# Two layers of graph attention in one launch: who copies the encoder's denominators, where the last attention's small tiles live, and in which order layer 1's squares and relus run

## The chip, the core and the metric

The kernel runs on one NeuronCore of a Trainium2 chip. A core has five engines that run side by side, each with its own queue of instructions in a fixed order: TensorE (PE in the profile, PEld its weight loads), VectorE (DVE), ScalarE (ACT), GpSimd (POOL) and SyncE (SP), the last two of which here mostly issue DMA transfers. Engines wait for each other through semaphores. The metric is the device time of one launch in microseconds; the median of three runs of the kernel before is 3309.0 us (3308.68 to 3311.59).

## What is computed

The graph has 4096 nodes with 512 features and an adjacency matrix of zeros and ones. Layer 0 is an encoder and a decoder with the same attention weights, each followed by a multilayer block with batch norm; layer 1 is a graph attention of four heads. Cut to what matters:

```python
# layer 0: h = relu(layernorm(x)), four heads of 128 features
Xw  = einsum('hnd,hde->hne', Xh, W)
sig = sigmoid(f1[:, :, None] + f2[:, None, :])       # f1, f2: Xw against two vectors per head
att = masked_softmax(adj * sig, adj != 0)            # rows sum to 1
Xc  = concat(att @ Xw)                               # encoder's attention
emb = mlp_block(batchnorm(Xc))
out = mlp_block(elu((att @ emb) @ W.T))              # decoder: the same att again
x   = x + out
# layer 1: h = relu(layernorm(x)), four heads
feats  = einsum('nf,hfo->hno', h, W1)
logits = leaky_relu(e_s[:, :, None] + e_n[:, None, :], 0.2)
x = x + relu(softmax(logits where adj else -1e10) @ feats + b)
```

## The kernel before

**Attention.** The function `attention` (line 210) is called three times: "enc", "dec" and "gat". It runs over 8 blocks, one for each head h and each half tb of the target nodes (2048 columns). A block has NJ = 32 steps, one for each 128 source nodes. In a step, ScalarE makes the unnormalised weights e of 128 sources by 2048 targets (lines 419 and 420 for enc and dec, line 798 for gat), VectorE multiplies them by the mask a (line 421 or 799), and TensorE adds four products of 512 columns to the output (line 351; line 348 for the first two steps of the fourth output bank). An f32 matmul stands as two records in the trace. The tiles e rotate through a fixed set of buffers: eight in the encoder, so that step j + 8 writes the buffer that step j used.

**Denominators.** The encoder and gat also need the sum of e over all sources. It is formed in three ways, by the tables at lines 62 to 64: some steps go to TensorE as products with ones (line 303), eleven of 32 are added up in memory by accumulating transfers that GpSimd issues (line 363, `acc<-e` in the encoder), the others are added by VectorE (lines 369 and 371). At the end of a block TensorE adds the three parts into one PSUM bank, `den`. Each accumulating transfer is issued after the one before it has landed. The buffer of e is free only once its transfer has landed.

**The end of a block, spread over the next.** At step 2 of the next block the output banks are copied out (line 520, VectorE). At step 4, `denominators` (line 244) copies `den` to SBUF, sends it to memory and back through GpSimd's queue (lines 248 and 250), and at step 10 it is inverted (line 254). The inverse comes back spread over partitions (line 261) and scales the outputs. In the encoder, every fifth e is stored for the decoder, which reads it back.

**Order.** A framework turns the Python order into one fixed order of instructions for each engine and lets a pool's tile wait for what used its memory before. `tc.issue_after(x)` and `pinned(list)` hold instructions behind others on this order.

**Layer 1's projection.** Line 705, `centred(ib)`, works on 512 nodes: it subtracts the mean over features (line 714), takes the relu into hT for TensorE (line 717), the square (line 719), and sums the squares over features (line 720). TensorE then forms the mean square (line 726), from which `deviation` makes the scale of the evictions (line 748). TensorE's projection is line 743. Small tiles are in the pools `l_small` and `l_work`, closed before the pool "gat" is opened on the same memory.

**Entry of the last attention.** Lines 762 to 789 find the largest score, broadcast it (mbc), exponentiate columns (jcol), sum the features (line 776), and store the target rows g (line 789) for later blocks. Row 0 is made ready inside the first step (lines 796 and 797), in four parts.

Of the kernel before, what the change touches and what calls it, by code (L numbers as in the profile page):

```python
# [80 lines left out]
def kernel(ctx, tc, x, xT, adjT, w0, w0T, v0, wencT, wdecT, vecs, w1, w1T, a1, outT):  # L81
# [21 lines left out]
    def bank1():  # L103
        return psum1.tile([P, IB], FP, name="den")
# [70 lines left out]

        return pv[:, 0:2 * DX].rearrange("p (h x) -> p h x", x=DX)

    def store_rows(dst, src):

        n = src.shape[-1]  # L180
        pr = bank1()
        nc.tensor.transpose(pr[0:n, 0:P], src, ident)
        fr = consts.tile([P, P], FP, name="fr")
        nc.vector.tensor_copy(fr[0:n, :], pr[0:n, 0:P])
        nc.scalar.dma_start(dst.rearrange("h (q p) -> (h q) p", p=P), fr[0:n, :])

    def targets(tb):
        return score[:, 0, tb].rearrange("p h q -> p (h q)")
# [21 lines left out]
    def attention(what, keep, pools, weights, values, row_of, out, finish, ebufs, modes=None, invert=None,  # L210
# [33 lines left out]
        def denominators(h, tb, den):  # L244

            dsb = spool.tile([P, IB], FP, name="dsb")
            nc.scalar.copy(dsb, den)
            nc.gpsimd.dma_start(dens[h][tb], dsb[0:P:32, :])
            dcol = spool.tile([P, TB // P], FP, name="dcol", bufs=2)
            nc.gpsimd.dma_start(dcol, dens[h][tb].rearrange("s (q k) -> (s q) k", k=TB // P))  # L250
            return dcol
# [41 lines left out]
        for n, (h, tb) in enumerate(blocks):  # L293
# [15 lines left out]
            for j in range(NJ):  # L309

                with pinned(products_of):
                    for f in later.pop(j, []):
                        f()
                with tc.issue_after(a_load.ins) if j else nullcontext():
                    if (n, j) in extras:
                        extras[n, j](a_load)
                    if not last and j == NJ - 10:
                        next_row = next_row_of(*blocks[n + 1])
                if n == 0 and moved and j == NJ - 2:
                    back = weight_tile()  # L320
                    nc.gpsimd.dma_start(back, dacc)
                e = weight_tile()
                store = j % KEEP == KEEP - 1 and kept is not None
                if store and kept == "read":
                    a_load = nc.sync.dma_start(e, ekeep[h][tb][j // KEEP])
                else:
                    if masks0:
                        a, a_load = masks0.pop(0)
                    else:
                        a = mask_tile(keep)  # L330
                        a_load = load_mask(a, tb, j)
                    products_of = weights(e, rowb, a, j, h, SB if n + j == 0 else 1)
                    if store:
                        stores.append((j // KEEP, e))

                    if j % KEEP == KEEP - 3 and stores:
                        k, t = stores.pop()
                        nc.scalar.dma_start(ekeep[h][tb][k], t)

                def products():  # L340
                    nonlocal last_main, last_ones

                    with tc.issue_after(last_ones.ins) if last_ones is not None else nullcontext():

                        if j == EVICT:
                            po.append(bank())
                            for k, t in ahead:
                                nc.tensor.matmul(po[-1], block(values[h], k), t[:, (SB - 1) * IB:SB * IB],  # L348
                                                 start=(k == 0), stop=False)
                        for s, b in enumerate(po):  # L350
                            last_main = nc.tensor.matmul(b, block(values[h], j), e[:, s * IB:(s + 1) * IB],  # L351
                                                         start=(j == 0), stop=(j == NJ - 1))
                    last_ones = None


                early = last and j == NJ - 1 and invert is not None
                if not early:
                    products()
                if j < EVICT:
                    ahead.append((j, e))  # L360
                if invert is not None:
                    if j in moved:
                        nc.gpsimd.dma_start(sums2 if n else dacc, e, **({"accum_op": ALU.add} if j > moved[0] else {}))  # L363
                    elif j in by_ones:
                        held.append(e)
                    else:
                        adds.append(e)
                        if len(adds) == 2:
                            nc.vector.tensor_add(acc, *adds)
                        elif len(adds) > 2:  # L370
                            nc.vector.tensor_add(acc, acc, e)  # L371

                    if held and j + 1 not in by_ones:
                        with tc.issue_after(last_main.ins):
                            for t in held:
                                add_to_den(t)
                        held = []
                    if j == NJ - 1:
                        with tc.issue_after(last_ones.ins) if last_ones is not None else nullcontext():
                            if moved:  # L380
                                add_to_den(sums2 if n else back)
                            add_to_den(acc, True)
                if early:
                    products()
# [260 lines left out]


    v1 = xd
    with tc.tile_pool(name="l_small", bufs=1) as small, tc.tile_pool(name="l_work", bufs=2) as work:
        x1 = [R[2]] + [small.tile([P, N], FP, name=f"x1_{o}") for o in range(1, C)]

# [49 lines left out]
            nc.vector.tensor_copy(w1x[:, :, :, D:DX], pw[:, 0:2 * C * H].rearrange("p (c h s) -> p c h s", h=H, s=2))  # L700
        mean_of = small.tile([P, P], FP, name="mean_of")
        nc.gpsimd.memset(mean_of, 1.0 / F)
        vacc = small.tile([P, H, D], FP, name="vacc")

        def centred(ib):

            if ib >= NIB // 2:
                residual(C - 2, ib)
            residual(C - 1, ib)
            pm = bank()  # L710
            nc.tensor.matmul(pm, mean_of, S[ib], start=True, stop=True)
            sq = work.tile([P, C, IB], FP, name="sq", bufs=1)
            for fb in range(C):
                nc.vector.tensor_sub(sq[:, fb, :], nodes(x1[fb], ib), pm)
            hT = work.tile([P, C, IB], FP, name="hT")
            for fb in range(C):
                nc.scalar.activation(hT[:, fb, :], sq[:, fb, :], AF.Relu)  # L717
            for fb in range(C):
                nc.scalar.activation(sq[:, fb, :], sq[:, fb, :], AF.Square)
            nc.vector.tensor_reduce(S[ib], sq.rearrange("p c n -> p n c"), AX.X, ALU.add)  # L720
            return hT

# [36 lines left out]
                row0 = w.rearrange("p c f -> p (c f)")  # L759
                load_row(row0, rows1[0], 0)  # L760

        mloc = small.tile([P, H], FP, name="mloc")
        nc.vector.tensor_reduce(mloc, score[:, 1].rearrange("p t h q -> p h t q"), AX.XY, ALU.max)
        pt = bank1()
        nc.tensor.transpose(pt[0:H, 0:P], mloc, ident)
        mrow = small.tile([H, 1], FP, name="mrow")
        nc.vector.tensor_reduce(mrow, pt[0:H, 0:P], AX.X, ALU.max)
        mdiag = small.tile([H, H], FP, name="mdiag")
        nc.vector.tensor_scalar_mul(mdiag, ident[0:H, 0:H], mrow)
        pm = bank1()  # L770
        nc.tensor.matmul(pm[:, 0:H], ones[0:H, :], mdiag, start=True, stop=True)
        nc.vector.tensor_copy(mbc, pm[:, 0:H])

        pss = bank1()
        for h in range(H):
            last_sum = nc.tensor.matmul(pss[:, h:h + 1], vacc[:, h, :], ones[:, 0:1], start=True, stop=True)
        nc.vector.tensor_scalar_mul(ssum, pss[:, 0:H], TINY)
        mb = mbc.unsqueeze(1).unsqueeze(3).to_broadcast([P, NTB, H, NJ // NTB])
        nc.vector.tensor_sub(jcol, score[:, 1], mb)
        nc.scalar.activation(jcol2, jcol, AF.Exp, scale=0.2)  # L780
        nc.scalar.activation(jcol, jcol, AF.Exp)
        nc.vector.tensor_scalar_mul(nq, jcol2, -1.0)

        g = small.tile([P, NTB, H, NJ // NTB], FP, name="g")
        nc.vector.tensor_add(g, score[:, 0], mb)
        nc.vector.tensor_scalar_min(g, g, G_MAX)
        nc.scalar.activation(g, g, AF.Exp, scale=0.8)
        with tc.issue_after(last_sum.ins):
            store_rows(rowsg, g.rearrange("p t h q -> p (t h q)"))


    def gat_weights(e, rowb, a, j, h, parts):
        for e, rowb, a in in_parts(parts, e, rowb, a):

            if parts > 1:
                nc.vector.tensor_scalar(rowb, rowb, mbc[:, h:h + 1], G_MAX, ALU.add, ALU.min)
                nc.scalar.activation(rowb, rowb, AF.Exp, scale=0.8)
            last_act = nc.scalar.activation(e, rowb, AF.Relu, bias=column(nq, j, h), scale=column(jcol, j, h))  # L798
            last_dve = nc.vector.scalar_tensor_tensor(e, e, column(jcol2, j, h), a, ALU.add, ALU.mult)  # L799
        return last_act, last_dve  # L800
# [18 lines left out]
    with tc.tile_pool(name="gat", bufs=1) as spool:  # L819
        x1_last = []  # L820

        def load_last(load):
# [3 lines left out]
        attention("gat", spool, spool, gat_weights, v1, lambda h, tb: (rowsg, tb * H + h), out_gat,  # L826
                  (scaled_gat, add_to_output), 7, lambda n: GAT, (N * TINY, ALU.add), sums=R[2][:, 0:TB],
                  sums2=row0, row0=row0,
                  extras={(H * NTB - 1, NJ - 10): load_last})


def _inputs(x, adj, w):
# [39 lines left out]
```

## Time and profile before

The profiled run took 3310.35 us, with a span of 3308.6 us and a mean granted TensorE clock of 0.989. Busy times of stretches of the profile, in us:

| stretch (us from the start) | what | PE | DVE | ACT | DMA share |
|---|---|---|---|---|---|
| 452 to 574 (122) | one encoder block | 118.30 | 115.51 | 120.38 | 0.87 |
| 1500 to 2200 (700) | decoder's attention and the next block | 700.00 | 431.24 | 608.90 | 0.39 |
| 2200 to 2300 (100) | entry and first part of layer 1's projection | 93.79 | 70.64 | 62.14 | 0.23 |
| 2500 to 3000 (500) | last attention | 496.57 | 488.23 | 302.24 | 0.82 |

A stretch's busy time near its length marks an engine without slack there; three engines stand near it in the encoder. Matmuls are pipelined and their ends are modelled, so PE's figure overstates its load a little. Over the whole span PE is busy 98%, DVE 81%, ACT 79%.

### The profile page before, as it was taken

The numbers are of one execution on the slowest core, as the hardware profiler recorded it, in microseconds if no ns is written. First come the engines' busy times: TensorE is split into PE (matmuls) and PEld (weight loads), VectorE is DVE, ScalarE is ACT, GpSimd is POOL, SyncE is SP. The second block draws the span as 40 slices with busy tenths as digits, with TensorE's granted clock in tenths as the row PEclk, the third lists the DMA queues.
The fourth block names the chain that finished last, engine by engine and source line by source line (L and its number), as shares of the span: only waits on it lengthen the run. The fifth ranks groups of instructions, "written<-read, shape, count | busy, mean of one in ns | idle before, by whom it ended". The sixth has DMA issues, their size and how long they took to land.

```text
span 3308.6 us, 25868 instructions
## 1 busy us (share of the span) xinstructions
PE 3226.6 (98%) x8847; PEld 1492.2 (45%) x8847; DVE 2677.1 (81%) x1912; ACT 2602.9 (79%) x1908; POOL 329.1 (10%) x478
## 2 busy tenths in 40 slices
PE   7989999999999999999999999999999999999999
PEld 6434434434443464444444444448644444444443
DVE  6989899999998675555655666586599989999997
ACT  7999999999997448999999999565656566566563
POOL 2000110110110000000000000024201111111111
PEclk9999999999999999999999999999999999999999
DMA  9994888988986013333443443232389779778876
GB/s 207 196 187 147 249 225 231 248 224 227 248 238 186 4 45 137 135 129 137 152 140 124 137 153 133 66 134 75 82 199 223 174 194 221 192 193 208 216 190 147
DMA packets 180164, 558.54 MB, mean 169 GB/s; under 512 B 20356, under 2 KB 23684, under 8 KB 144192
## 3 DMA queue, kind: packets, MB, share of 16 engines
q0 software_dynamic: 43088, 210.09, 32.9%
q1 hardware_dynamic: 126288, 293.66, 26.2%
q10 hardware_dynamic: 10656, 53.15, 4.0%
q8 instruction: 69, 1.13, 0.1%
q14 instruction: 63, 0.52, 0.0%
HBM read 378.15 MB, written 95.82 MB: 143 GB/s over the span
## 4 chain that ended last, share of the span: by engine, by line
PE 67%; DVE 16%; issue 9%; ACT 5%; DMA 3%; DVEq 0%; ACTq 0%; POOL 0%; POOLq 0%
PE ps L351 52%; PE ps L566 7%; DVE e L421 4%; DVE e L799 4%; DVE R L371 4%; PE ps L743 3%; ACT e L419 2%; PE den L303 2%; DVE acc L371 2%; ACT e L420 2%; DMA a<-mask 2%; PE ps L622 1%; PE ps L348 1%; PE ps L500 1%; DMA rb<-rinvs 1%
## 5 line engine op out<-in xcount | busy, mean ns | idle before, releaser
L351 PE MATMUL ps<-e,R 128*128 128x512 f32 x6048 | 2640.7, 597 | 51.8 <-DVE e L421 39.9
L351 PEld LDWEIGHTS ps<-e,R 128*128 128x128 f32 x6048 | 1147.4, 191 | 1536.4 <-issue 1417.3
L421 DVE TENSOR_TENSOR e<-e,a 128x2048 f32<-128x2048 f32 (+1 forms) x470 | 1052.3, 2260 | 403.6 <-ACT e L420 381.6
L419 ACT ACTIVATE e<-rowb,score 128x2048 f32<-128x2048 f32 (+1 forms) x470 | 912.6, 1968 | 91.3 <-PE ps L351 58.0
L420 ACT ACTIVATE e<-e 128x2048 f32<-128x2048 f32 (+1 forms) x470 | 871.0, 1880 | 17.5 <-DVE e L421 11.1
L798 ACT ACTIVATE e<-rowb,nq,jcol 128x2048 f32<-128x2048 f32 x224 | 457.9, 2086 | 225.2 <-DMA w<-e 130.1
L799 DVE SCALAR_TENSOR_TENSOR e<-e,jcol,a 128x2048 f32<-128x2048 f32 (+1 forms) x259 | 591.5, 2319 | 4.5 <-DMA a<-mask 2.7
L371 DVE TENSOR_TENSOR R<-R,e 128x2048 f32<-128x2048 f32 x128 | 292.5, 2285 | 0.0
L371 DVE TENSOR_TENSOR acc<-acc,e 128x2048 f32<-128x2048 f32 x126 | 287.9, 2285 | 1.8
L566 PE MATMUL ps<-R,w 128*128 128x512 f32 x512 | 220.3, 592 | 0.6 <-DVE w L534 0.6
L261 POOL DMA_DIRECT2D rb<-rinvs x88 | 58.7, 683 | 1095.6 <-DVE R L524 904.8
L566 PEld LDWEIGHTS ps<-R,w 128*128 128x128 f32 x512 | 97.2, 190 | 122.7 <-issue 118.2
L363 POOL DMA_DIRECT2D w<-e x77 | 64.6, 839 | 643.6 <-DMA w<-e 267.5
L743 PE MATMUL ps<-w1x,hT 128*128 128x260 f32 x512 | 119.6, 393 | 1.8 <-ACT hT L717 1.8
L586 ACT ACTIVATE ex<-ps,bias 128x512 f32<-128x512 f32 x64 | 44.0, 688 | 95.5 <-PE ps L566 78.4
L363 POOL DMA_DIRECT2D acc<-e x66 | 55.6, 842 | 607.7 <-DMA acc<-e 225.7
L743 PEld LDWEIGHTS ps<-w1x,hT 128*128 128x128 f32 x512 | 99.2, 195 | 22.0 <-ACT hT L717 3.4
L798 ACT ACTIVATE e<-w,nq,jcol 128x2048 f32<-128x2048 f32 (+1 forms) x35 | 65.6, 1938 | 30.1 <-DMA dacc<-e 28.6
L811 ACT ACTIVATE R<-R,vec 128x512 f32<-128x512 f32 x32 | 23.0, 719 | 72.4 <-DVE R L808 72.3
L588 DVE SCALAR_TENSOR_TENSOR ex<-ex,re 128x512 f32<-128x512 f32 x64 | 45.0, 703 | 35.7 <-ACT re L587 35.5
L748 ACT ACTIVATE R<-ps,rstd 128x128 f32<-128x128 f32 x128 | 38.0, 367 | 42.4 <-PE ps L743 42.4
L303 PE MATMUL den<-e,ones 128*32 128x512 f32 x584 | 70.9, 599 | 0.0
(158 smaller groups left out, 1265.1 us busy)
## 6 DMA issues: line engine op xcount, KB each, us to landing
a<-mask SPq DMA_DIRECT2D x720, 256.0 KB, 3.5
w<-e POOLq DMA_DIRECT2D x77, 1024.0 KB, 8.2
acc<-e POOLq DMA_DIRECT2D x66, 1024.0 KB, 8.6
ekeep<-e ACTq DMA_DIRECT2D x48, 1024.0 KB, 5.5
e<-ekeep SPq DMA_DIRECT2D x48, 1024.0 KB, 4.9
rb<-rinvs POOLq DMA_DIRECT2D x88, 256.0 KB, 5.7
mask<-in_adjT POOLq DMA_DIRECT2D x8, 2048.0 KB, 103.3
rowb<-rows SPq DMA_DIRECT2D x16, 1024.0 KB, 4.9
```

What stands on the lines that cost most here:

```text
L261: nc.gpsimd.dma_start(rb, everywhere(rinvs[h][tb], 0, s * IB, IB))
L303: last_ones = nc.tensor.matmul(den[s * 32:(s + 1) * 32, :], ones[:, 0:32], t[:, s * IB:(s + 1) * IB], start=not begun, stop=stop)
L351: last_main = nc.tensor.matmul(b, block(values[h], j), e[:, s * IB:(s + 1) * IB], start=(j == 0), stop=(j == NJ - 1))
L363: nc.gpsimd.dma_start(sums2 if n else dacc, e, **({"accum_op": ALU.add} if j > moved[0] else {}))
L371: nc.vector.tensor_add(acc, acc, e)
L419: nc.scalar.activation(e, rowb, AF.Tanh, bias=column(score[:, 1], j, h), scale=0.5)
L420: last_act = nc.scalar.activation(e, e, AF.Exp, scale=0.5)
L421: last_dve = nc.vector.tensor_mul(e, e, a)
L566: nc.tensor.matmul(z, w[:, fb, o * P:(o + 1) * P], nodes(src[fb], ib), start=(fb == 0), stop=(fb == C - 1))
L743: nc.tensor.matmul(b[:, 0:2 * DX], hT[:, fb, c * P:(c + 1) * P], w1x[:, fb, 2 * k:2 * k + 2, :].rearrange("p h x -> p (h x)"), start=(fb = ...
L798: last_act = nc.scalar.activation(e, rowb, AF.Relu, bias=column(nq, j, h), scale=column(jcol, j, h))
L799: last_dve = nc.vector.scalar_tensor_tensor(e, e, column(jcol2, j, h), a, ALU.add, ALU.mult)
```

## The change

It has four parts. (1) In the encoder, the copy of `den` goes to VectorE instead of ScalarE; gat keeps ScalarE. (2) Small tiles that are used around the entry of the last attention (vacc, mloc, mrow, mdiag, g) go into a pool "edge" that stays open, so that the first tiles of "gat" don't wait for their last users; row 0 is made ready ahead of the attention, and the feature sums and rows g are computed from within it, at step 1 (`rest_of_rows`), g stored by SyncE's queue. (3) In `centred`, from the second group of nodes on the centred values go straight to hT, each square is issued ahead of its relu, and the relu works in place; the first group keeps relus first. (4) `store_rows` takes a bank of the rotating seven instead of the single `den` bank, and extras of a step are held behind the step's own weights.

```diff
-    def store_rows(dst, src):
+    def store_rows(dst, src, queue=nc.scalar):
...
-        pr = bank1()
+        pr = bank()
...
-        nc.scalar.dma_start(dst.rearrange("h (q p) -> (h q) p", p=P), fr[0:n, :])
+        queue.dma_start(dst.rearrange("h (q p) -> (h q) p", p=P), fr[0:n, :])
...
             dsb = spool.tile([P, IB], FP, name="dsb")
-            nc.scalar.copy(dsb, den)
+            (nc.vector.tensor_copy if kept is not None else nc.scalar.copy)(dsb, den)
...
-                with tc.issue_after(a_load.ins) if j else nullcontext():
+                with pinned([a_load, *products_of] if j else []):
                     if (n, j) in extras:
...
+    edge = ctx.enter_context(tc.tile_pool(name="edge", bufs=1))
...
-        vacc = small.tile([P, H, D], FP, name="vacc")
+        vacc = edge.tile([P, H, D], FP, name="vacc")
...
+            hT = work.tile([P, C, IB], FP, name="hT")
             sq = work.tile([P, C, IB], FP, name="sq", bufs=1)
+
+            d = hT if ib else sq
             for fb in range(C):
-                nc.vector.tensor_sub(sq[:, fb, :], nodes(x1[fb], ib), pm)
-            hT = work.tile([P, C, IB], FP, name="hT")
+                nc.vector.tensor_sub(d[:, fb, :], nodes(x1[fb], ib), pm)
             for fb in range(C):
-                nc.scalar.activation(hT[:, fb, :], sq[:, fb, :], AF.Relu)
-            for fb in range(C):
-                nc.scalar.activation(sq[:, fb, :], sq[:, fb, :], AF.Square)
+                if ib:
+                    nc.scalar.activation(sq[:, fb, :], d[:, fb, :], AF.Square)
+                nc.scalar.activation(hT[:, fb, :], d[:, fb, :], AF.Relu)
+            if ib == 0:
+                for fb in range(C):
+                    nc.scalar.activation(sq[:, fb, :], d[:, fb, :], AF.Square)
...
-        pss = bank1()
-        for h in range(H):
-            last_sum = nc.tensor.matmul(pss[:, h:h + 1], vacc[:, h, :], ones[:, 0:1], start=True, stop=True)
-        nc.vector.tensor_scalar_mul(ssum, pss[:, 0:H], TINY)
...
-        nc.scalar.activation(jcol, jcol, AF.Exp)
+        last_act = nc.scalar.activation(jcol, jcol, AF.Exp)
...
+        for row, in in_parts(SB, row0):
+            last_dve = nc.vector.tensor_scalar(row, row, mbc[:, 0:1], G_MAX, ALU.add, ALU.min)
+            with tc.issue_after(last_act.ins):
+                last_act = nc.scalar.activation(row, row, AF.Exp, scale=0.8)
+
+    def rest_of_rows(load):
+
+        pss = bank()
+        for h in range(H):
+            nc.tensor.matmul(pss[:, h:h + 1], vacc[:, h, :], ones[:, 0:1], start=True, stop=True)
+        nc.vector.tensor_scalar_mul(ssum, pss[:, 0:H], TINY)
...
+        store_rows(rowsg, g.rearrange("p t h q -> p (t h q)"), nc.sync)
...
-            if parts > 1:
-                nc.vector.tensor_scalar(rowb, rowb, mbc[:, h:h + 1], G_MAX, ALU.add, ALU.min)
-                nc.scalar.activation(rowb, rowb, AF.Exp, scale=0.8)
...
-                  extras={(H * NTB - 1, NJ - 10): load_last})
+                  extras={(0, 1): rest_of_rows, (H * NTB - 1, NJ - 10): load_last})
```

More of the change, by code (lines that the diff above doesn't have):

```diff
@@ L760 @@
                 load_row(row0, rows1[0], 0)
-        mloc = small.tile([P, H], FP, name="mloc")
+        mloc = edge.tile([P, H], FP, name="mloc")
         nc.vector.tensor_reduce(mloc, score[:, 1].rearrange("p t h q -> p h t q"), AX.XY, ALU.max)
@@ L765 @@
         nc.tensor.transpose(pt[0:H, 0:P], mloc, ident)
-        mrow = small.tile([H, 1], FP, name="mrow")
+        mrow = edge.tile([H, 1], FP, name="mrow")
         nc.vector.tensor_reduce(mrow, pt[0:H, 0:P], AX.X, ALU.max)
-        mdiag = small.tile([H, H], FP, name="mdiag")
+        mdiag = edge.tile([H, H], FP, name="mdiag")
         nc.vector.tensor_scalar_mul(mdiag, ident[0:H, 0:H], mrow)
@@ L780 @@
         nc.scalar.activation(jcol2, jcol, AF.Exp, scale=0.2)
-        nc.scalar.activation(jcol, jcol, AF.Exp)
+        last_act = nc.scalar.activation(jcol, jcol, AF.Exp)
         nc.vector.tensor_scalar_mul(nq, jcol2, -1.0)
-        g = small.tile([P, NTB, H, NJ // NTB], FP, name="g")
+        for row, in in_parts(SB, row0):
[7 more added lines that the diff above has]
+        nc.vector.tensor_scalar_mul(ssum, pss[:, 0:H], TINY)
+        g = edge.tile([P, NTB, H, NJ // NTB], FP, name="g")
         nc.vector.tensor_add(g, score[:, 0], mb)
@@ L787 @@
         nc.scalar.activation(g, g, AF.Exp, scale=0.8)
-        with tc.issue_after(last_sum.ins):
-            store_rows(rowsg, g.rearrange("p t h q -> p (t h q)"))
+        store_rows(rowsg, g.rearrange("p t h q -> p (t h q)"), nc.sync)
     def gat_weights(e, rowb, a, j, h, parts):
         for e, rowb, a in in_parts(parts, e, rowb, a):
-            if parts > 1:
-                nc.vector.tensor_scalar(rowb, rowb, mbc[:, h:h + 1], G_MAX, ALU.add, ALU.min)
-                nc.scalar.activation(rowb, rowb, AF.Exp, scale=0.8)
             last_act = nc.scalar.activation(e, rowb, AF.Relu, bias=column(nq, j, h), scale=column(jcol, j, h))
```

## The prediction, made before the changed kernel ran

> **What bounds the kernel now.** I read the chain of waits first, then busy times by stage, then each engine's waits, then single instructions around the places the change touches. The chain of the page runs mostly through TensorE:
>
> ```profile
> PE 67%; DVE 16%; issue 9%; ACT 5%; DMA 3%; DVEq 0%; ACTq 0%; POOL 0%; POOLq 0%
> ```
>
> The windows (length, then busy time and instructions of PE, PEld, DVE, ACT and POOL, granted clock, DMA share, GB/s), for one encoder block, the decoder, the second group of layer 1's projection and the entry of gat:
>
> ```profile
> 452.00:574.00 122.00, 118.30 (x305) 50.06 (x304) 115.51 (x63) 120.38 (x66) 13.21 (x18) 0.99 0.87 233
> 1300.00:1350.00 50.00, 50.00 (x118) 22.11 (x117) 25.21 (x11) 46.82 (x28) 0.00 (x0) 1.00 0.30 100
> 2250.00:2255.00 5.00, 5.00 (x16) 3.85 (x15) 1.81 (x5) 0.91 (x4) 2.08 (x3) 0.66 0.57 159
> 2363.00:2376.00 13.00, 7.43 (x16) 3.98 (x17) 6.96 (x15) 9.60 (x13) 0.56 (x1) 0.50 0.47 154
> ```
>
> In the encoder ScalarE is the fullest; the decoder is TensorE alone, so nothing that VectorE or ScalarE does can pay there, and the change leaves its order alone; at the last two places TensorE is idle in part and its clock has fallen. Waits by engine in the encoder (engine and work that waits, whom for, sum, count, longest):
>
> ```profile
> ACT dsb L247 <- PE den L303: 19.6, 7, 5.2
> DVE e L421 <- ACT e L420: 42.9, 28, 2.5
> POOL acc L363 <- DMA acc<-e: 225.7, 25, 11.8
> ```
>
> ScalarE has one wait per block, for the denominator bank; VectorE waits for ScalarE's weights; the accumulating transfers wait for one another all the time.
>
> **What the Trainium skill says.** [...] VectorE is at 115.51, so there is room for a copy and not for much more. "DMA: Bandwidth & Descriptors", section "Two DMAs through the same engine are not ordered", says that a dependent transfer has to be held until the first one's semaphore shows it complete. This is what makes the accumulates a serial chain; in the trace each is issued some 0.5 us after the one before has landed, and lands 4.6 to 11.4 us later. "TensorE: Matmul & The Clock Gate", section "What's actually happening", says that the array falls to half clock after an idle window of about 3.4 us and comes back after a busy one; the trace agrees, with 0.50 and 0.66 in the two windows above.
>
> **Part 1, the encoder's copy: what it frees.** Single instructions of ScalarE at the seam of two blocks (start, duration, line, tiles, shape, count, and in brackets the wait ahead):
>
> ```profile
> 574.55 3.69 ACT L420 ACTIVATE e<-e 128x2048 f32<-128x2048 f32 x2
> 581.00 0.59 ACT L247 COPY dsb<-den 128x512 f32<-128x512 f32 x1 [2.75 <-PE den L303]
> 581.48 3.90 ACT L419 ACTIVATE e<-rowb,score 128x2048 f32<-128x2048 f32 x2
> ```
>
> The seven waits (19.6) and seven copies of 0.58 make 23.7 us that ScalarE would not spend. The first block's 5.0 of it lies beside a start that is held by mask transfers, so 18.6 is the most that can come out, if ScalarE alone bounds. A block takes 121.46 us on the mean; ScalarE without wait and copy, 118.8.
>
> **What it costs VectorE.** The same shape, 128x512 f32 from PSUM, is the copy of L520:
>
> ```profile
> 576.69 2.48 DVE L520 COPY R<-ps 128x512 f32<-128x512 f32 x4
> ```
>
> Four in 2.48, so 0.62 each. "VectorE: DVE Perf Modes", section "The TRN2 errata", gives 120 + FD/Accel cycles at 0.96 GHz, which for 512 at factor 1 is an estimate of 0.66; I take the trace's 0.62. That makes 114.8 + 0.6 = 115.4 of VectorE's work a block, below any period in question. Does the copy wait there? In the built order it stands behind the weights of the next block's step 3. VectorE is there at 462.7 in block 3, and the bank is complete at 458.84. So no wait: behind it would be the weights of step 4, for which TensorE waits, but there is 3.9 us to spare, and earlier ScalarE work brings VectorE forward by less than that.
>
> **What takes ScalarE's place.** Not all of 18.6 arrives, because of the buffers. Eleven tiles per block leave through the accumulate chain, and step 25 of ScalarE writes the buffer that step 17's transfer reads. Single instructions of GpSimd and ScalarE in block 3:
>
> ```profile
> 526.53 0.85 POOL L363 DMA_DIRECT2D acc<-e  x1 [10.50 <-DMA acc<-e]
> 536.88 0.86 POOL L363 DMA_DIRECT2D acc<-e  x1 [8.93 <-DVE e L421]
> 580.41 0.55 POOL L363 DMA_DIRECT2D acc<-e  x1 [23.14 <-PE den L303]
> 581.88 0.58 POOL L248 DMA_DIRECT2D dens<-dsb  x1 [0.92 <-ACT dsb L247]
> ...
> 537.39 3.88 ACT L419 ACTIVATE e<-rowb,score 128x2048 f32<-128x2048 f32 x2
> ```
>
> The transfer of step 17 (issued at 526.53) lands at 536.35, and ScalarE starts step 25 at 537.39: 1.04 to spare. In blocks 4 to 6 it is 0.92, 1.35 and 0.38, and for step 22's transfer before step 30 it is 0.12 to 1.95. The chain starts anew in each block when TensorE has finished the last sums (580.41 above), which is itself late only because ScalarE and VectorE are. So the chain closes a loop over two blocks: from its start to the landing of step 17, 78.15 (mean of 78.03, 78.16, 77.73, 78.69); plus 0.55, because the changed order puts the send of the denominators (L248) behind the second accumulate of a block and delays the third by one issue (in gat, where such a send stands between two, the next accumulate goes out 1.07 after the landing instead of 0.53); plus 0.08 to ScalarE's start of step 25; plus 76.05 from there to step 14 of the next block (79.38 and 78.12 in the trace, each less its wait and copy); plus 85.1 from there through VectorE, which is continuous from step 13 on, to the next start (85.73 and 84.46). The sum is 239.93 for two blocks, 120.0 a block: a gain of 1.46, not 2.7. I take 1.46 for blocks 3 to 6. Block 2, where ScalarE waits 4.43 + 0.58 and the slack is larger, I put at 4 (TensorE's idle time there). Block 7 is VectorE's in its second half, and the batch norm's coefficients go out a step later; 0.6. Sum 4 + 4 x 1.46 + 0.6 = 10.4, with 4 (the chain slower under more crowding) and 18.6 as ends.
>
> **Part 3, squares first.**
>
> ```profile
> 2244.46 3.74 DVE L720 TENSOR_REDUCE S<-sq 128x512 f32<-128x2048 f32 x1 [1.39 <-ACT sq L719]
> 2248.35 1.02 PE L726 MATMUL den<-mean_of,S 128*128 128x1 f32 x8 [1.21 <-DVE score L749]
> ```
>
> The sum of squares starts when the last square is done, and TensorE stands 1.21 for it. The squares go ahead of relus, so the last one ends about 1.9 earlier: the 1.39 of VectorE and the 1.21 of TensorE go, and with the idle time the dip to 0.66 in 2250 to 2255, worth 1.7. At most 2.9; I take 2, since an earlier dip can remain. The relus are late by as much, but TensorE needs hT only at 2249.23. The remaining groups are under TensorE's work.
>
> **Part 2, the entry of gat.**
>
> ```profile
> 2366.42 28.61 SPq L199 DMA_DIRECT2D a<-mask  x13
> 2369.75 2.08 DVE L799 SCALAR_TENSOR_TENSOR e<-e,jcol,a 128x512 f32<-128x512 f32 x3 [2.74 <-DMA a<-mask]
> 2370.60 5.46 PE L351 MATMUL ps<-e,R 128*128 128x512 f32 x6 [4.25 <-DVE e L799]
> ```
>
> TensorE has ended the projection at 2360.0 and starts the attention at 2370.60, because the masks, issued at 2366.42 behind the old users of their memory, hold VectorE for 2.74. With the pool "edge" the masks come earlier, and the row's exponentials (ScalarE, four quarters at 2363.7 to 2365.8, then the quarters of e to 2368.6) decide: the first product at about 2367.35, 3.25 earlier. Against that, the sums (1.66, L776) and the transposition of g (0.47) now stand behind step 0's first products, in TensorE's queue: 3.25 - 2.13 = 1.1, and perhaps 1 more if the half clock ends sooner. I take 1.5, between 0 and 3.5. Queued behind the sums are step 0's last product and step 1's; the copy of ssum is on VectorE behind step 1's weights, where only step 2 waits. Gat's TensorE has little slack afterwards, so this carries to the end. Store queue and rowsg are needed only by block 1: nothing. Part 4 at the front is hidden by mask transfers: nothing, give or take 1.
>
> **Sum.** 10.4 + 2 + 1.5 = 13.9; 3309.0 - 13.9 = 3295.1, so 3295.
>
> **Rivals.** (A) ScalarE alone bounds the encoder, since the accumulates shorten with an earlier rhythm (they land in 4.6 when alone): 18.6 + 2.9 + 3.3 = 24.8 at most, with 2 and 1.5 it is 22.1, so 3287 (3284 to 3290). For it: the chain idles 23 us at each block's end. Against it: the margins of 0.12 to 1.35 above. (B) The chain, pushed closer, slows (DMA share is 0.87 already) and takes nearly all: encoder 5, layer 1 1, gat 0: 3303. For it: POOL's 225.7 of waiting; against it: the chain's 78 us varied by under 1 us over four blocks. (C) Slower: VectorE, second fullest, takes the wait with the copy, because its order lets it reach the bank early: ScalarE's 2.8 a block becomes VectorE's, and VectorE's continuous second half starts that much later, 7 x (2.8 + 0.62) = 23.9 less 3.5 of parts 2 and 3: 3329. Against it: 3.9 us to spare at 462.7. A mild form is VectorE bound by 0.62 a block, 4.3, about the size of the other gains: no change, 3309.
>
> **Chances.** Forecast 0.52, A 0.25, B 0.13, C 0.10 with its mild form. Range: 3285 leaves out a corner of A, 3303 leaves out C and a little of B, some 2 in 10 in all. The bound of 0.2% lies at 3302.4: forecast, A and half of B are faster, 0.84; the other half of B and mild C the same, 0.09; C 0.07.
>
> **What would show it.** Right: no wait on L247 and no copy on ScalarE in the encoder; the copy of some 0.6 on VectorE without a wait; a block of some 120 us; a new ScalarE wait at L419 for a DMA of `acc<-e` at step 25 or 30, of 0.5 to 2 us; no TensorE wait at the mean squares of the second group; the first product of gat about 3 us sooner after the projection. Blocks near 118.8 without such waits would show A; blocks over 121 with long waits on the chain, B; a DVE wait for `den`, C. What would make it wrong above all: a chain of accumulates that changes its pace with its timing.

## The result: 3296.5 us, and the profile after

The changed kernel takes 3296.51 us (median of six runs, 3290.74 to 3298.19), the kernel before 3308.88 beside it; the ratio is 0.9959 with a 95% interval of 0.9946 to 0.9972. The forecast was 3295. The profiled run has a span of 3294.5 us, 14.1 below that of before. Where this came from is read by comparing the same points of both traces (us):

| stretch | before | after | difference |
|---|---|---|---|
| start to the end of the encoder's attention | 1075.03 | 1061.79 | -13.24 |
| decoder's attention, first to last product | 887.39 | 889.07 | +1.68 |
| layer 1's projection, first to last product | 131.08 | 131.49 | +0.41 |
| from there to the last attention's first product | 10.62 | 7.56 | -3.06 |
| last attention and tail | 938.0 | 938.1 | +0.1 |

The encoder made the gain, although its block 1 began 1.2 later than before. In detail, by ScalarE's first step of each block (blocks are counted from 0): block 2 took 124.51 and takes 120.47; blocks 3 to 6 took 485.85 together and take 475.36, or 118.84 each.

The chain of waits of the page leans a little less on TensorE:

```profile
PE 63%; DVE 16%; issue 9%; ACT 7%; DMA 4%; DVEq 0%; POOL 0%; ACTq 0%; SPq 0%; POOLq 0%
```

Windows of the changed kernel (columns as before), for one encoder block, the projection's third group and the entry of the last attention:

```profile
439.50:558.30 118.80, 116.27 (x305) 49.66 (x304) 114.64 (x65) 118.67 (x66) 13.24 (x18) 1.00 0.86 236
2253.00:2260.00 7.00, 5.88 (x29) 4.88 (x30) 2.92 (x12) 1.75 (x7) 3.48 (x9) 1.00 0.19 75
2349.00:2362.00 13.00, 6.28 (x19) 3.40 (x20) 8.96 (x20) 11.78 (x17) 1.42 (x3) 0.74 0.50 185
```

ScalarE works 118.67 of 118.80: it has no time left. VectorE, with the copy, is at 114.64, and TensorE at 116.27. In the 13 us after the projection's last product the granted clock is 0.74; from the same point of before it is 0.61 (the 0.50 of the window shown before starts 3 us later). Waits in the encoder, of VectorE, of GpSimd and of ScalarE:

```profile
DVE e L421 <- ACT e L420: 23.7, 12, 2.2
POOL acc L363 <- DMA acc<-e: 178.6, 23, 10.1
ACT e L419 <- DMA acc<-e: 0.7, 2, 0.5
```

ScalarE's wait for the denominators is gone, and what the forecast put in its place, a wait for the accumulates, is 0.7 us in all. That isn't so in every execution. A second profile of the same kernel, taken with the later runs below, has more of it:

```profile
ACT e L419 <- DMA acc<-e: 2.9, 5, 1.0
```

There block 3 takes 118.75 again, but blocks 4 to 6 take 119.80 to 119.82, and in each of these ScalarE waits 0.8 to 0.95 for an accumulate, near step 17 or at step 25. At the seam of two blocks ScalarE runs through, and VectorE makes the copy in 0.68 without a wait (single instructions of the first profile, of ScalarE, then of VectorE):

```profile
558.27 3.88 ACT L419 ACTIVATE e<-rowb,score 128x2048 f32<-128x2048 f32 x2
...
578.37 0.68 DVE L247 COPY dsb<-den 128x512 f32<-128x512 f32 x1
```

### The profile page after: what moved, and what is told of

Its sections match the earlier page's. It is cut to its first block, busy times and chain, and to the rows that moved or that the text cites. A ratio compares the mean times of both kernels' runs of the same rounds, so it can differ in the third digit from the quotient of the medians.

```text
span 3294.5 us, 25880 instructions
## 1 busy us (share of the span) xinstructions
PE 3215.3 (98%) x8847; PEld 1489.2 (45%) x8847; DVE 2682.0 (81%) x1919; ACT 2598.9 (79%) x1901; POOL 331.2 (10%) x478
## 4 chain that ended last, share of the span: by engine, by line
PE 63%; DVE 16%; issue 9%; ACT 7%; DMA 4%; DVEq 0%; POOL 0%; ACTq 0%; SPq 0%; POOLq 0%
PE ps L351 49%; PE ps L566 7%; DVE e L421 6%; ACT e L419 4%; DVE e L808 3%; PE ps L750 3%; DMA a<-mask 3%; DVE R L371 3%; ACT e L420 2%; DVE acc L371 2%; PE den L303 1%; PE ps L622 1%; PE ps L348 1%; DMA rb<-rinvs 1%; PE ps L500 1%
## 5 line engine op out<-in xcount | busy, mean ns | idle before, releaser
L421 DVE TENSOR_TENSOR e<-e,a 128x2048 f32<-128x2048 f32 (+1 forms) x470 | 1051.7, 2259 | 386.3 <-ACT e L420 364.3
L419 ACT ACTIVATE e<-rowb,score 128x2048 f32<-128x2048 f32 (+1 forms) x470 | 912.9, 1968 | 100.1 <-PE ps L351 58.1
L420 ACT ACTIVATE e<-e 128x2048 f32<-128x2048 f32 (+1 forms) x470 | 871.1, 1880 | 17.1 <-DVE e L421 10.9
L363 POOL DMA_DIRECT2D w<-e x77 | 64.7, 841 | 641.2 <-DMA w<-e 254.5
L750 PE MATMUL ps<-w1x,hT 128*128 128x260 f32 x512 | 118.4, 391 | 1.8 <-ACT hT L723 1.8
L363 POOL DMA_DIRECT2D acc<-e x66 | 55.8, 845 | 572.4 <-DMA acc<-e 178.6
L750 PEld LDWEIGHTS ps<-w1x,hT 128*128 128x128 f32 x512 | 98.6, 194 | 21.6 <-ACT hT L723 3.4
L755 ACT ACTIVATE R<-ps,rstd 128x128 f32<-128x128 f32 x128 | 38.4, 368 | 38.3 <-PE ps L750 37.4
```

The costliest lines, as they stand in the source:

```text
L419: nc.scalar.activation(e, rowb, AF.Tanh, bias=column(score[:, 1], j, h), scale=0.5)
L420: last_act = nc.scalar.activation(e, e, AF.Exp, scale=0.5)
L421: last_dve = nc.vector.tensor_mul(e, e, a)
L750: nc.tensor.matmul(b[:, 0:2 * DX], hT[:, fb, c * P:(c + 1) * P], w1x[:, fb, 2 * k:2 * k + 2, :].rearrange("p h x -> p (h x)"), start=(fb = ...
```

## The experiments

All times are medians beside runs of the kernel before on the same chip (3310.1 to 3311.0). Lines of a trace bear the line numbers of the kernel that ran. In the changed kernel they are the printed ones up to line 644; behind it, L671 and L675 are the printed lines 669 and 673 (residual adds), L727 is 720 (sum of squares), L733 is 726 (mean squares) and L750 is 743 (projection).

### One part at a time

**The copy alone**, on the kernel before:

```diff
-            nc.scalar.copy(dsb, den)
+            (nc.vector.tensor_copy if kept is not None else nc.scalar.copy)(dsb, den)
```

> The kernel before with one edit: the encoder's copy of the denominator bank goes to VectorE. Theory 1 (ScalarE alone bounds the encoder, and the accumulate chain moves with it): blocks 3 to 6 take 118.8 us each as in the changed kernel, the encoder's attention ends 13 to 14.5 us earlier than before, and the whole kernel is 11 to 15 us faster than before. Theory 2 (the forecast's loop over two blocks, with the rest of the measured gain from other parts of the change): blocks of 120.0, about 10 us in the encoder. Theory 3 (the copy alone does little; the held-back extras or the bank of store_rows free the encoder): under 5 us.

Measured: 3296.63 us, ratio 0.9959 (0.9944 to 0.9974), the same as the whole change. Blocks 3 to 6 take 118.75 each, and the encoder's attention ends at 1060.73, 14.3 earlier than before. So neither part 4 nor another part is needed for the gain. One of these blocks as a window:

```profile
439.09:557.84 118.75, 116.83 (x305) 49.51 (x305) 114.61 (x65) 118.62 (x66) 13.26 (x18) 1.00 0.88 239
```

**The copy taken back**, all else as changed (the edit above, reversed):

> The changed kernel with the encoder's copy given back to ScalarE. Theory 1: blocks of 121.4 as before, ScalarE waits again for TensorE's denominators (about 19 us in 7 waits), the encoder's attention ends at 1075 or, with the front 1.2 us later as in the changed kernel, at 1076; in all 0 to 4 us faster than before (the entry of the last attention gives 3). Theory 3: the encoder keeps over half of its gain of 13.

Measured: 3312.0 us, 1.0005 (0.9997 to 1.0014). Blocks 3 to 6 take 122.1 (121.46 before; 121.4 was expected), and the wait is back:

```profile
ACT dsb L247 <- PE den L303: 21.3, 7, 4.4
```

So one line holds the whole measured gain; parts 2 to 4 together give none that shows in the time.

**Squares ahead of relus alone**, and later the changed kernel **with relus first again**. The edit of the first is part 3 of the diff on the kernel before; that of the second is the same, reversed, on the changed kernel.

> The kernel before with one edit: squares ahead of relus in layer 1 from the second group on, as in the change. Theory 1 (the residual adds that wait for the features' transfers take the place of the squares): TensorE's wait at the second group's mean squares goes from 1.2 to about 0.4, a wait of about 1.5 appears at the third group's, and from the projection's first to its last product it takes 131 to 132 us, as before (131.1); in all no difference, -1 to +1 us. Theory 2 (the forecast: 2 us gained here, and the third group's wait comes from the pool of the small tiles): 129 us from first to last, no wait at the third group.

> The changed kernel with layer 1's relus first again (part 3 undone, everything else kept). Theory (part 3 costs some 2 us, as the projections show: 129.6 to 131.1 with relus first, 131.4 to 133.5 with squares first): 129 to 131 us for the projection, 1 to 2.5 us faster than the changed kernel. Rival (the forecast: part 3 gains): slower than the changed kernel by 1 to 2 us.

Measured: 3311.16 us alone (1.0003, 0.9995 to 1.0012), and 3295.53 with part 3 undone, beside 3296.04 for the changed kernel on the same chip (0.9959 and 0.9958 to before). Neither way shows a difference in the time. The projection by itself leans the other way than forecast: it took 131.56 with squares alone and 130.59 with part 3 undone, against 131.38 for the changed kernel beside it. Over all profiles but those of the last experiment, four with relus first took 129.60 to 131.09, and seven with squares first 131.17 to 133.51 (stretches of half clock, as the one of 1.7 before, are in some of both). The wait that squares should remove falls from 1.21 to 0.36 at the second group of nodes, and another one comes at the third. TensorE and VectorE there, in the changed kernel:

```profile
2254.12 1.05 PE L733 MATMUL den<-mean_of,S 128*128 128x1 f32 x8 [1.48 <-DVE S L727]
...
2243.26 0.71 DVE L671 TENSOR_TENSOR x<-x,xt 128x512 f32<-128x512 f32 x1 [1.65 <-DMA xt<-in_xT]
2249.73 0.69 DVE L675 TENSOR_TENSOR S<-S,x 128x512 f32<-128x512 f32 x1 [1.17 <-POOL S L675]
2250.34 3.72 DVE L727 TENSOR_REDUCE S<-sq 128x512 f32<-128x2048 f32 x1
```

VectorE's sum for the third group stands behind residual adds of later groups (L671, L675), which wait for a transfer of features and for GpSimd. In the new order on VectorE the subtractions of a group come ahead of such an add (in the traces, at the second group), so the add, and the load that reuses its buffer, come later. The last experiment tests this.

**The entry of the last attention alone**: part 2 on the kernel before.

```diff
-        vacc = small.tile([P, H, D], FP, name="vacc")
+        vacc = edge.tile([P, H, D], FP, name="vacc")
...
+                  extras={(0, 1): rest_of_rows, (H * NTB - 1, NJ - 10): load_last})
```

> The kernel before with one edit: the pool edge, row 0 made ready ahead, sums and rows g inside step 1 of the last attention. Theory 1 (the masks come early and TensorE's idle time ends sooner, and with it the half clock): no mask wait at the first weights, first product 7.5 us after the projection's last (10.6 before), step 1's products 3 us sooner, in all 2 to 4 us faster. Theory 2 (the forecast's sum: sums and transposition in TensorE's way take 2.1 back): 1 to 1.5 us. Rival (the gain belongs to the order of squares and relus, which frees engines at the projection's end): nothing.

Measured: 3308.61 us, 0.9994 (0.9985 to 1.0003). The first product comes 7.55 after the projection's last, as in the changed kernel. The thirty-first product record comes 23.60 after it; before it was 26.63, but 25.70 in both runs (the copy alone, the squares alone) that have the old entry, so 2.1 of the 3.0 hold against those too. The interval reaches over 1: on its own this gain can't be told from none.

### Does ScalarE alone bound the encoder?

**Four copies more on ScalarE**, which wait for nothing:

```diff
+            if kept is not None:
+                junk = spool.tile([P, P], FP, name="junk")
+                for _ in range(4):
+                    nc.scalar.copy(junk, rowb[:, 0:P])
```

> The changed kernel with four copies of 128x128 f32 from SBUF to a tile that nobody reads added to ScalarE in each of the encoder's blocks 1 to 7, at step 4 and after; they wait for nothing. It adds their own time alone, and separates ScalarE's work from its wait for the bank. Theory 1 (ScalarE alone bounds): the blocks 3 to 6 grow by just the copies' time on ScalarE, about 1.0 to 1.5 us each, and the encoder's attention ends 6 to 9 us later than in the changed kernel. Theory 2 (the loop through the accumulates bounds at a fixed pace): under 0.3 us a block, since ScalarE would have slack.

Measured: 3300.26 us. The copies are shorter than I had put them, 0.18 to 0.20 each from start to start, 0.8 a block, and the blocks 3 to 6 take 119.55 to 119.57, which is 0.80 more than 118.76. Each bit of ScalarE's time is a bit of the block's: in the window of block 3, ScalarE is busy 119.42 of 119.55. The encoder's attention ends 3.5 later than in the first profile of the changed kernel.

### How near is the accumulate chain, and what made it shorter?

**The third accumulate held** by a second store of the denominators' rows:

```diff
             nc.gpsimd.dma_start(dcol, dens[h][tb].rearrange("s (q k) -> (s q) k", k=TB // P))
+            if kept is not None:
+                nc.gpsimd.dma_start(dens[h][tb], dsb[0:P:32, :])
```

> The changed kernel with a second store of the denominators' rows put behind their load on GpSimd's queue in the encoder's blocks 1 to 7. It has to wait until the load has landed, and holds the third accumulate of the block by some 2 us. It writes the same values again. Theory 1a (the chain has its margin of 0.1 to 1.2 us at step 25 and no more, its transfers take what they take): ScalarE waits 1 to 2 us for a transfer at steps 17 to 30 of each block, blocks of 120 us, the encoder 5 to 8 us longer. Theory 1b (the chain is elastic: later transfers meet less of the row load and take less, as steps 15 and 17 did in the changed kernel): margins stay above 0 at nearly all steps, and the blocks stay at 118.8 to 119.2.

Measured: 3310.7 us, 0.9999 (0.9990 to 1.0007): the gain is gone. The hold was larger than I had put it: in block 3 the third accumulate goes out 18.67 after the first, instead of 14.43. ScalarE's waits, and GpSimd's instructions at the hold (L421 and L365 here are L419 and L363 of the changed kernel; the profiled execution took 3316.93, above the median, so its waits may be too):

```profile
ACT e L421 <- DMA acc<-e: 22.9, 13, 4.8
...
481.96 0.56 POOL L252 DMA_DIRECT2D dens<-dsb  x1 [3.64 <-DMA dcol<-dens]
482.51 0.95 POOL L365 DMA_DIRECT2D acc<-e  x1
```

So the loop of the forecast exists, and 4.2 us more in it cost as much as the copy had gained. The chain isn't elastic enough to take up such a delay. In the changed kernel it only lies just short of ScalarE, or, in blocks 4 to 6 of the second profile, a little beyond it.

**The row load moved by two steps**, to see what a transfer's duration hangs on:

```diff
-                    if not last and j == NJ - 10:
+                    if not last and j == NJ - (8 if kept is not None else 10):
```

> The changed kernel with the load of the next block's row, 1 MB on SyncE's queue, behind the mask of step 23 or 24 instead of that of step 21, in encoder and decoder; nothing else moves. Theory 1b (the chain became 3 us shorter because the row load no longer lies on the transfer of step 15): the load now lies on steps 15 and 17, these take 10 to 11.5 us each instead of 8.4 and 8.9, ScalarE waits 1 to 3 us per block for a transfer at step 25, and the encoder is 5 to 10 us longer than in the changed kernel. Rival (the shortening came from elsewhere, as from the order of the second accumulate and the denominators' store): the chain at 75 us, no such waits, same time as the changed kernel.

Measured: 3300.57 us, 0.9973 (0.9964 to 0.9982), 4.5 slower than the changed kernel beside it. Three kernels tell the story, each with the issue of the row load on SyncE's queue and the accumulates on GpSimd's. Before:

```profile
512.36 0.45 SPq L192 DMA_DIRECT2D rowb<-rows  x1
514.61 0.85 POOL L363 DMA_DIRECT2D acc<-e  x1 [9.61 <-issue]
```

The load lands at 520.46, so it lies on the transfer of step 15, issued at 514.61, which takes 11.39 us. In the changed kernel ScalarE is early and the load with it (it stands on SyncE's queue behind mask loads, which wait for VectorE's use of older masks, and that follows ScalarE), while the chain starts at nearly the same place of the block:

```profile
507.25 1.29 SPq L192 DMA_DIRECT2D rowb<-rows  x1
...
513.50 0.85 POOL L363 DMA_DIRECT2D acc<-e  x1 [9.87 <-DVE R L524]
522.42 0.85 POOL L363 DMA_DIRECT2D acc<-e  x1 [7.50 <-DMA acc<-e]
```

The load lands at 516.09, after 2.6 us of step 15's transfer, which takes 8.39. Blocks 4 to 6 show the same: before, one transfer in each has the row load on it and takes 11.6 to 12.1; in this profile of the changed kernel none takes over 10.7, with the load spread over the seam of two. With the load two steps later it is step 17's turn:

```profile
516.80 1.35 SPq L192 DMA_DIRECT2D rowb<-rows  x1
...
521.43 0.85 POOL L363 DMA_DIRECT2D acc<-e  x1 [7.63 <-DVE e L421]
534.57 0.85 POOL L363 DMA_DIRECT2D acc<-e  x1 [11.71 <-DMA acc<-e]
...
534.12 3.90 ACT L419 ACTIVATE e<-rowb,score 128x2048 f32<-128x2048 f32 x2 [0.56 <-DMA acc<-e]
```

It takes 12.61 us (8.87 in the changed kernel), and ScalarE waits for it at step 25: in blocks 2, 3, 5 and 6 by 0.56 to 2.27, in block 4 by 0.12. From its start to the landing of step 17 the chain takes 77.4 to 79.5 in blocks 3 to 6; the mean is 75.2 in the first profile of the changed kernel and 76.6 in the second. Step 15's transfer was quick here (8.53), unlike my expectation, although the load lay on it for 4.1 us and on step 17's for 5.9. So the place of the row load sets the chain's length in part, but the time that the two share doesn't alone say how long a transfer becomes.

### A version that is faster than both

**The third group's sum first**: the residual adds of the fourth to the eighth group are held behind the sum of squares of the group before.

```diff
+            behind = reduces[-1] if ib > 2 else None
-            residual(C - 1, ib)
+            residual(C - 1, ib, behind)
...
+            with tc.issue_after(behind.ins) if behind is not None else nullcontext():
                 nc.vector.tensor_add(d, d, xt)
```

> The changed kernel with the residual adds of layer 1's groups 3 to 7 held behind the sum of squares of the group before, so that the sum of the third group does not stand behind adds that wait for transfers. Theory (these adds are what gave the gain of part 3 back): TensorE's wait of 1.5 at the third group's mean squares goes, the projection takes 129 to 130 us from first to last product instead of 131.5, in all 1.5 to 2.5 us faster than the changed kernel. Rival (TensorE would wait for the next thing, the means over features or the squares themselves): a wait of 1 us or more appears at another group, and 131 to 132 us as before.

> The kernel of the run reduce_first once more, beside the changed kernel. Theory: 1.5 to 2.5 us faster than the changed kernel, projection at 129 to 130. Rival (its 3291 was the luck of one chip): the same as the changed kernel.

> The changed kernel itself, beside the next two on one chip. Expected: 13 to 14 us faster than the kernel before, blocks 3 to 6 of the encoder at 118.8, the projection of layer 1 at 131 to 133 us from first to last product.

Measured: 3291.11 us the first time (0.9936 to before, 0.9921 to 0.9952). The second time, beside the changed kernel, 3292.13 against 3296.04 (0.9948, 0.9936 to 0.9961, against 0.9958, 0.9946 to 0.9971). The last two intervals overlap; over both times the nine runs took 3287.05 to 3293.48, and eleven runs of the changed kernel 3290.74 to 3298.19. All that TensorE waits in the projection of the first profile is, by its groups of waits (L755 is the projection here, L182 a transposition):

```profile
PE ps L755 <- ACT hT L727: 1.8, 1, 1.8
PE ps L182 <- DVE score L761: 1.3, 1, 1.3
```

The wait of 1.48 is gone, and the projection takes 129.44 and 130.17, against 131.49 and 131.38 in the changed kernel's two profiles. That is 1.2 of the 3.9 us of the second time. The rest of the difference between the two profiles lies where the edit changes nothing that I can name: the encoder's attention ends 2.4 earlier, the decoder's takes 1.2 longer, and the last attention takes 906.8 from its thirty-first product record to its last against 909.6. Two profiles of the changed kernel differ in the last by 2.5 (912.1 and 909.6), so I hold the part in the projection for shown and leave the rest open.

## Why the prediction came out right, and which of its steps did not

**The time** was right, but by luck: two errors of opposite sign cancelled. The sum was 10.4 + 2 + 1.5. The copy alone gave 13.7 (3310.29 to 3296.63), 3.3 more than forecast, and the other parts, forecast at 3.5, gave nothing that shows in the time. By stages, the first profile has 13.2 in the encoder, nothing from part 3, some 2 to 3 at the entry, and +1.7 in the decoder, which I had not put in.

**The copy's cost** held: 0.68 for one, without a wait, VectorE at 114.6 and never the bound. Rival C had nothing for it: the bank is always complete when VectorE arrives.

**The encoder's gain**: block 2 was put at 4 and gave 4.04 (its wait for the bank was 5.18; the 4.43 that the prediction reads there is block 1's). Blocks 3 to 6 were put at 1.46 each and gave 2.62 (485.85 less 475.36, by four). The step that failed is the loop over two blocks, in its first term: 78.15 us from the chain's start to the landing of step 17, carried over unchanged. In the first profile of the changed kernel it is 74.75, 75.24, 74.86 and 75.97 in blocks 3 to 6, and with the copy alone 75.28 to 76.09. The second term was right: the order of the sends delays the third accumulate by 0.56 on the mean of the four blocks (14.52 after the first instead of 13.96), against 0.55. With 75.2, which has that delay in it, in place of 78.15 + 0.55 the loop gives 118.2, just below ScalarE's 118.8, and ScalarE is the bound. In the second profile the chain takes 74.56, 76.67, 77.53 and 77.46, and in blocks 4 to 6 the forecast's wait stands in the trace, with 0.8 to 0.95 us a block; these blocks gain some 1.65 on the mean of before, near the forecast's 1.46. So the loop exists, and its first term was mis-sized.

Rival A, at 0.25, was right on the first profile and on the copy alone. Its reason, that the accumulates shorten with an earlier rhythm, came true only in the sense of a changed collision. I had taken the sum of eight durations from the trace without asking which other transfer lay on each (they run up to 12.1 in blocks 3 to 6; the 11.4 that the prediction gives is block 3's). Step 15's transfer, mostly the one under the row load, is shorter by 2.1 on the mean of blocks 3 to 6, the largest part of the 2.9; that load is timed by ScalarE and not by the chain, and moving it brought the waits back. It isn't the whole: steps 10 and 17 are shorter by 1.1 and 1.2, step 7 is longer by 1.6, and with the copy alone block 5 still has the load on step 15 for 5.5 us (11.00) and a chain of 76.09. What sets those durations is open. The last sentence of the prediction names such a chain as what would make it wrong.

**The margin** was right as a fact. In the first profile ScalarE starts step 25 only 0.11 to 0.99 us after the landing of step 17, in the second it waits, and the run with the held chain lost the whole gain.

**Part 3** was put at 2 and gave nothing in the time; the projection by itself became longer rather than shorter (131.17 to 133.51 against 129.60 to 131.09). The step that failed is "The remaining groups are under TensorE's work": I looked at the group where the wait was, and not at what the next groups had waiting behind it. Also, the 1.7 for the clock's dip was no property of the order: the run with the copy alone has the same wait of 1.2 at the second group and a granted clock of 1.00 there, and its projection takes 129.91.

**The entry** went as worked out up to the first product, 3.06 sooner (3.25 forecast) between the two profiles; two other profiles with the old entry have 9.48 and 9.52 in place of 10.62, so 2.0 of it hold against these. The sums and the transposition take 1.0 of TensorE behind step 0's products instead of 2.13, and the granted clock is at 1 again there (half clock ends at 2359.7, the sums start at 2360.68). In the profiled run all 3.0 remain, and about 2 against other runs of the old entry; 1.5 was forecast.

**The decoder's +1.68** is half clock near TensorE's first stop there, of 2.56 us, which both kernels have: the granted clock stands at 0.50 for 6.83 us before and for 10.24 in the changed kernel, and 3.41 us more at half clock cost 1.7. In thirteen profiles of all kernels this attention took 887.4 to 889.1 us; one and the same kernel, the last one above, took 887.4 in one profile and 889.1 in another, so it is no effect of the change. The same holds for the front: block 1 begins at 184.6 to 192.1 in these profiles, without a pattern by part 4.

## What to carry to other kernels

A wait in front of a short operation belongs to the operation: moving a copy of 0.6 us to an engine that reaches it later took 2.6 us a block off the fullest engine, most of it the wait. A serial chain of transfers need not keep its duration (this one took 78.2 before and 75.2 or 76.6 after, on the mean of four blocks); before carrying one over to a changed rhythm, list for each transfer which other one lies on it and which engine times that one. Compare more than one profile where two bounds lie within 1 us of each other. And after a wait is removed in a pipelined loop, look at the same wait one and two turns later, since a queue with a fixed order may have put the next delay just there.

## What the runs showed of the hardware that I had not expected

- In blocks 3 to 6 of all thirteen profiles, a transfer of 1 MB that accumulates takes 4.6 to 5.8 us as the first of a block. Step 15's takes 10.9 to 11.8 where another 1 MB load, the row, lies on it for 5.4 us or more, and 8.4 to 9.0 where that is 2.4 to 3.3. Step 17's takes 8.4 to 11.0 without the row load and 12.6 to 13.8 with it. Without a row load transfers of steps 5 to 10 still reach 12.1, so this load isn't the only cause of a long one.
- The same wait of 1.2 us of TensorE led to half clock in one profile (0.66 over 5 us) and to none in another (1.00 over 8 us), so a gap of this length had no fixed price. Half clock came in stretches of 3.41 us and multiples of it (6.83, 10.24, 13.65), the one at the end of each trace apart. The prediction takes from the Trainium skill, "TensorE: Matmul & The Clock Gate", section "What's actually happening", that half clock follows an idle window of about 3.4 us; the length agrees, but in the 3.41 us ahead of two such stretches of the kernel before (at 2250.46 and 2363.10) TensorE stood idle for only 1.21 and 2.27.
- VectorE's residual add of 128x512 takes 0.68 us, but 1.70 to 1.74 where GpSimd's add of the same shape, 1.26 to 1.28 us, runs beside it (L671 and L675 of the changed kernel), and 1.45 where the two share 0.9 us only. The Trainium skill, "Perfetto Trace Analysis", section "Optimizing Scalar/DVE Operations", says that the two share a port to SBUF; the trace agrees, though no run here separated the two adds.
